# Small VectorE steps of the attention's shifts and output layernorms, queued and issued between row maxima

## The chip, the cores and the metric

The kernel runs on one core of one Trainium2 chip. The metric is the device time of one execution in microseconds. The kernel before took 1540.59 us, the median of three runs (1538.79, 1540.59 and 1546.41).

## What is computed

The reference is a stack of two layers on x with 2 x 1024 tokens of 512 features, all in float32. Each layer has an attention part and a feed-forward part, and each part is put between two layernorms:

```python
x = x + _layernorm(_L0_attn_ref(_layernorm(x), ...))   # per-token attention over feature groups
x = x + _layernorm(_L0_ffn_ref(_layernorm(x), ...))    # weights quantized to -1, 0, 1
x = x + _layernorm(_L1_attn_ref(_layernorm(x), ...))   # causal attention, 16 heads, 4 key/value heads, rope
x = x + _layernorm(_L1_ffn_ref(_layernorm(x), ...))    # gated, 2 of every 4 hidden values kept
```

The change is in the third line. Its core is

```python
logits = jnp.einsum('bhqd,bhkd->bhqk', q, k_ctx) / math.sqrt(dk)     # dk = 32, T = 1024
probs = jax.nn.softmax(logits + mask, axis=-1)
out = jnp.einsum('bhqk,bhkd->bhqd', probs, v_ctx)
return out.transpose(0, 2, 1, 3).reshape(Bx, Tx, D_MODEL) @ c_w.T
```

and then the layernorm of that output is added to x.

## The kernel before, in words

Tokens lie on the 128 partitions, 16 tiles of 128 tokens (8 for each of the two batches), four tiles to a group. The first two parts of the stack run until about 400 us of the profiled execution, the causal attention until about 957 us, and the last feed-forward part from there to the end.

**Tasks and steps of the attention.** A task is one batch b, one group of query tokens Q (0 or 1, 512 tokens each) and one key/value head g (0 to 3, which serves four query heads, REP = 4): 16 tasks. A task passes twice over its scores.

- *Row maxima and sums.* score_step (from L820) takes a tile of 128 queries (ii) and a chunk of up to 512 keys (ch). For each of the four heads TensorE multiplies (L830; the causal mask is added by a small matmul, L836), VectorE takes the negated row maximum from PSUM (L841, tile mxs), and ScalarE computes exponentials with that maximum as bias, keeping only their sum (L845, tile junk).
- *Shifts.* When a task has all its maxima and sums, shifts (from L880) makes of them one number per query and head, the minus logarithm of the denominator. With two key chunks it first combines them (mfin, md, an exponential of md on ScalarE at L890, sfin); minus_log computes a logarithm out of 14 VectorE steps on 128 x 16 values (L860 to L876); in_pieces splits the result into three bf16 pieces (L791 to L794, tile pm). That makes 18 VectorE steps for a task with Q = 0 and 22 for one with Q = 1. maxima_T (pieces_T, L801 and L803) transposes the pieces on TensorE and copies them to mT.
- *Probabilities and values.* prob_step j computes the transposed scores of one tile of 128 keys for the four heads (L906, pst), adds the shift by a short matmul with mT (L913), and ScalarE takes the exponential (L919, pT); GpSimd zeroes what the causal mask forbids (L921). value_step, one step later, multiplies by the values (L935, po) and at the end of a task copies the sum out (L943, oT).

**Output parts.** After the last task of a (b, Q) come output_parts: four products with the output weights (L969, py), for each a copy, bn_stats and bn_aggr on VectorE (L982 to L984), and then add: the inverse root of the variance out of 13 small VectorE steps on 128 x 4 values (inverse_root, L188 to L195), four ln_apply (L199, 128 x 512, tile tmpy) and four additions to x_sb on GpSimd (L962). The last (b, Q) is done tile by tile instead ("alone").

**What sets the order.** The main loop runs over 96 steps, one prob_step each. In a step it issues prob_step, then as many score steps of later tasks as are due (scores_up_to; a value_step goes between the first two heads and the last two), and then what was put on the list due for this step: projections of batch 1's queries, pieces of weights for the next stage, output_parts, maxima_T. Many steps have no score step. The loop stands in a manual schedule for TensorE and GpSimd: their instructions stay in the order of the program. VectorE's and ScalarE's order is chosen by the scheduler of the framework. GpSimd's additions of a layernorm are held back (soon) until the next prob_step has been issued (flush). Scores and transposed scores share a ring of seven PSUM banks, so that a score matmul waits until ScalarE has read the bank that it takes over.

Of the kernel before, what the change touches and what calls it, by code (L numbers as in the profile page):

```python
# [9 lines left out]
F32 = mybir.dt.float32  # L10
# [8 lines left out]
P = 128  # L19
# [5 lines left out]
def two_layer_sandwich(  # L25
# [138 lines left out]
    load_x(2 * GT, NT)  # L164


    def ln_stats(pool, srcs, name, roots=True):

        n = len(srcs)
        st = pool.tile([P, n, 6], F32, tag=f"st{n}", name=f"st_{name}")  # L170
        mv = pool.tile([P, n, 2], F32, tag=f"mv{n}", name=f"mv_{name}", bufs=4)
        rs = pool.tile([P, n], F32, tag=f"rs{n}", name=f"rs_{name}", bufs=4)
        for k, s in enumerate(srcs):
            nc.vector.bn_stats(out=st[:, k, :], in_=s)
            nc.vector.bn_aggr(out=mv[:, k, :], in_=st[:, k, :])
        if roots:
            nc.scalar.activation(rs, mv[:, :, 1], AF.Sqrt, bias=eps_t)
            nc.vector.reciprocal(rs, rs)
            return mv, rs
        return mv, inverse_root(pool, mv, n, name, rs)  # L180

    def inverse_root(pool, mv, n, name, rs=None):

        if rs is None:
            rs = pool.tile([P, n], F32, tag=f"rs{n}", name=f"rs_{name}", bufs=4)
        v = pool.tile([P, 2, n], F32, tag=f"nv{n}", name=f"nv_{name}", bufs=1)
        y = pool.tile([P, n], I32, tag=f"ny{n}", name=f"ny_{name}", bufs=1)
        nc.vector.tensor_scalar(v[:, 0, :], mv[:, :, 1], EPS_LN, None, ALU.add)  # L188
        nc.vector.tensor_scalar(y, v[:, 0, :].bitcast(I32), 1, None, ALU.logical_shift_right)
        nc.vector.tensor_scalar(rs.bitcast(I32), y, -1.0, 1597463007.0, ALU.mult, ALU.add)  # L190
        nc.vector.tensor_scalar(v[:, 0, :], v[:, 0, :], -0.5, None, ALU.mult)
        for _ in range(3):
            nc.vector.tensor_tensor(v[:, 1, :], rs, rs, ALU.mult)
            nc.vector.tensor_tensor(v[:, 1, :], v[:, 1, :], v[:, 0, :], ALU.mult)
            nc.vector.scalar_tensor_tensor(rs, v[:, 1, :], 1.5, rs, ALU.add, ALU.mult)  # L195
        return rs

    def ln_apply(dst, src, mv, rs, k):
        nc.vector.tensor_scalar(  # L199
            dst, src, mv[:, k, 0:1], rs[:, k : k + 1], ALU.subtract, ALU.mult  # L200
        )

    def minus_mean(pool, mv, rs, n):

        nb = pool.tile([P, n], F32, tag=f"nb{n}", name=f"nb{n}", bufs=4)
        nc.vector.scalar_tensor_tensor(nb, mv[:, :, 0], -1.0, rs, ALU.mult, ALU.mult)
        return nb

    def transpose4(src, pt):
# [575 lines left out]
    def in_pieces(m, name):  # L785

        nonlocal n_pm
        pm = pms[n_pm % 2]
        n_pm += 1
        r1 = s1.tile([P, GT, REP], F32, tag="r1", name=f"r1_{name}")  # L790
        nc.vector.tensor_copy(pm[:, :, :, 0], m)  # L791
        nc.vector.tensor_tensor(r1, m, pm[:, :, :, 0], ALU.subtract)
        nc.vector.tensor_copy(pm[:, :, :, 1], r1)
        nc.vector.tensor_tensor(pm[:, :, :, 2], r1, pm[:, :, :, 1], ALU.subtract)  # L794
        return pm

    def pieces_T(pm, name):
# [23 lines left out]
    def score_step(tk, ii, ch, heads):  # L821


        st, g, i = tk.st, tk.g, GT * tk.Q + ii
        k0 = ch * GW
        k1 = min(k0 + GW, (i + 1) * P)
        w = k1 - k0
        for r in heads:
            pa = ring(f"psc_{tk.nm}_{ii}_{ch}_{r}")
            nc.tensor.matmul(  # L830
                pa[:, :w], tk.q.bitcast(F32R)[:, r, ii * P : (ii + 1) * P],
                st.k[ch].bitcast(F32R)[:, g, :w],
                start=True, stop=True,
            )
            if k1 == (i + 1) * P:
                nc.tensor.matmul(  # L836
                    pa[:, w - P : w], identb, cmaskb, start=False, stop=True,
                    skip_group_check=True,
                )
            mx = tk.mx[:, ii, r, ch : ch + 1]  # L840
            nc.vector.tensor_reduce(mx, pa[:, :w], AX.X, ALU.max, negate=True)  # L841
            junk = s1.tile(
                [P, GW], BF16, tag="junk", name=f"junk_{tk.nm}_{ii}_{ch}_{r}", bufs=3
            )
            nc.scalar.activation(  # L845
                junk[:, :w], pa[:, :w], AF.Exp, bias=mx, accum_out=tk.sm[:, ii, r, ch : ch + 1]
            )
# [3 lines left out]
    def minus_log(v, m, name):  # L851


        def tmp(tag, dtype=F32):
            return s1.tile([P, GT, REP], dtype, tag=tag, name=f"{tag}_{name}", bufs=1)

        vi = v.bitcast(I32)
        e, f = tmp("lge", I32), tmp("lgf", I32)
        ef, z, z2, p = tmp("lgw"), tmp("lgz"), tmp("lgy"), tmp("lgp")
        nc.vector.tensor_scalar(e, vi, 23, None, ALU.logical_shift_right)  # L860
        nc.vector.tensor_scalar(
            f, vi, 0x7FFFFF, 0x3F800000, ALU.bitwise_and, ALU.bitwise_or
        )
        fr = f.bitcast(F32)
        nc.vector.tensor_scalar(ef, e, -LN2, 126.5 * LN2, ALU.mult, ALU.add)
        nc.vector.tensor_scalar(z, fr, R2, None, ALU.add)
        nc.vector.reciprocal(z, z)
        nc.vector.scalar_tensor_tensor(z, fr, R2, z, ALU.subtract, ALU.mult)
        nc.vector.tensor_tensor(z2, z, z, ALU.mult)
        nc.vector.tensor_scalar(p, z2, 1.0 / 9.0, 1.0 / 7.0, ALU.mult, ALU.add)  # L870
        nc.vector.tensor_tensor(p, p, z2, ALU.mult)
        nc.vector.scalar_tensor_tensor(p, p, 1.0 / 5.0, z2, ALU.add, ALU.mult)
        nc.vector.scalar_tensor_tensor(p, p, 1.0 / 3.0, z2, ALU.add, ALU.mult)
        nc.vector.scalar_tensor_tensor(p, p, 1.0, z, ALU.add, ALU.mult)
        nc.vector.scalar_tensor_tensor(ef, p, -2.0, ef, ALU.mult, ALU.add)
        nc.vector.tensor_tensor(ef, ef, m, ALU.add)  # L876
        return ef

    def shifts(tk):

        m, sm = tk.mx[:, :, :, 0], tk.sm[:, :, :, 0]
        if tk.Q > 0:
            n = tk.Q + 1
            m = s1.tile([P, GT, REP], F32, tag="mfin", name=f"mfin_{tk.nm}")
            nc.vector.tensor_reduce(m, tk.mx[:, :, :, :n], AX.X, ALU.min)
            d = s1.tile([P, GT, REP, n], F32, tag="md", name=f"md_{tk.nm}")
            nc.vector.tensor_tensor(
                d, m.unsqueeze(3).to_broadcast([P, GT, REP, n]), tk.mx[:, :, :, :n], ALU.subtract
            )
            nc.scalar.activation(d, d, AF.Exp)  # L890
            nc.vector.tensor_tensor(d, d, tk.sm[:, :, :, :n], ALU.mult)
            sm = s1.tile([P, GT, REP], F32, tag="sfin", name=f"sfin_{tk.nm}")
            nc.vector.tensor_reduce(sm, d, AX.X, ALU.add)
        tk.pm = in_pieces(minus_log(sm, m, tk.nm), tk.nm)

    def maxima_T(tk):
        tk.mT = pieces_T(tk.pm, tk.nm)

    def prob_step(tk, j):
# [45 lines left out]
    def output_parts(st, Q):  # L945
# [9 lines left out]
            return s1.tile([P, D], F32, tag=tag, name=f"tmp{nm}_{ii}", bufs=1)  # L955

        def add(tiles, mv, ys):
            rs = inverse_root(s1, mv, n, f"{nm}_{tiles[0]}")
            for k, ii in enumerate(tiles):
                ln_apply(ys[ii], py_of.pop(ii) if alone else ys[ii], mv, rs, k)  # L960
                xt = x_sb[:, st.b * TB + GT * Q + ii, :]
                soon(lambda xt=xt, y=ys[ii]: nc.gpsimd.tensor_tensor(xt, xt, y, ALU.add))  # L962

        py_of, got = {}, []

        def part(ii):
            py = py_of[ii] = ring(f"p{nm}_{ii}")
            for c in range(DC):
                nc.tensor.matmul(  # L969
                    py, st.oT[Q][:, c, ii * P : (ii + 1) * P], wc1[:, c, :],  # L970
                    start=(c == 0), stop=(c == DC - 1),
                )
            ys[ii] = y_of(ii)
            if not got or alone:
                got[:] = [
# [79 lines left out]
    with tc.manual_schedule(engines={mybir.EngineType.PE, mybir.EngineType.Pool}):  # L1055
# [84 lines left out]
        def f1_begin():  # L1140
# [4 lines left out]
            load_unit(1)  # L1145
            f1_first.xT = w1a.tile([P, DC, GW], F32, tag="xT", name="xTg1_0")
            f1_first.xd = w1a.tile([P, 3, 2, HW], F32, tag="xd", name="xdg1_0")
            f1_first.mv, f1_first.rs = ln_stats(s1, [x_sb[:, k, :] for k in range(GT)], "f1_0", roots=False)

        def f1_tile(k):  # L1150
# [24 lines left out]
        for step, (tk, j) in enumerate(t_steps):  # L1175
# [7 lines left out]
            def between():  # L1183
                while waiting:
                    waiting.pop()()

            scores_up_to(wanted(step), step, between)
            between()
            for f in due.pop(step, []):
                f()  # L1190
        values(len(t_steps))
        while due:
            step = min(due)
            flush()
            for f in due.pop(step):
                f()
# [426 lines left out]
```

## Time and profile before

| what | before |
|---|---|
| median of three runs | 1540.59 us |
| the profiled execution, its own time | 1545.5 us |
| its span, first to last instruction | 1543.8 us |
| mean granted TensorE clock | 0.968 |
| 0 to 400 us: TensorE, VectorE, ScalarE, GpSimd busy | 382.3, 234.0, 137.7, 139.5 us |
| 400 to 957 us (attention): the same | 508.2, 373.7, 393.7, 152.2 us |
| 957 us to the end: the same | 575.5, 402.4, 196.9, 28.7 us |
| row maxima (L841) | 384, 551 ns each |
| exponentials of scores (L845) and of pst (L919) | 384 of 630 ns, 384 of 551 ns |
| GpSimd additions of a normed tile (L962) | 16, median 1440 ns |

The table's busy times are sums of the durations of the instructions of an engine in that stretch. A busy TensorE is not TensorE at its full rate, since the clock that is granted to it can be half, and then each matmul takes longer. PE stands for TensorE, PEld for its weight loads, DVE for VectorE, ACT for ScalarE, POOL for GpSimd. A line such as L841 is a line of the kernel before.

### The profile page before, as it was taken

What the parts mean: (1) busy time and instruction counts of PE and PEld (TensorE: products, weight loads), DVE (VectorE), ACT (ScalarE), POOL (GpSimd) and SP (SyncE); (2) the same over time, 40 slices, a digit from 0 to 9 for tenths busy, and PEclk for the clock granted to TensorE, in tenths of its full rate; (3) what the DMA queues carried; (4) which work ended last, traced back from release to release, by engine and by line L of the source; (5) the groups of instructions that cost most, each with busy time, mean ns of one, the idle gap of its engine ahead of it and who ended that gap; (6) DMA issues with size and microseconds to landing.
All of it is one profiled execution on the core that took longest, in us unless ns stands there. A gap on an engine that the chain in (4) does not pass through costs nothing.

```text
span 1543.8 us, 20277 instructions
## 1 busy us (share of the span) xinstructions
PE 1466.0 (95%) x6998; PEld 1051.8 (68%) x6998; DVE 1010.0 (65%) x2303; ACT 728.2 (47%) x1849; POOL 320.4 (21%) x424
## 2 busy tenths in 40 slices
PE   7999999999779999999898999999999999999997
PEld 3558888877545554545444446888888888888886
DVE  5976465652467767657777645786578468846783
ACT  4242343332268757797685983451245034404420
POOL 1104475332303314323432002000100010001001
PEclk9999999999879999998798999999999999999999
DMA  7200211201554343343351002643353345235411
GB/s 293 75 14 28 82 55 42 55 18 52 122 151 101 104 124 89 117 135 74 93 148 57 2 1 88 247 144 143 130 211 117 143 171 191 96 143 205 156 48 75
DMA packets 78870, 167.51 MB, mean 109 GB/s; under 512 B 10224, under 2 KB 35824, under 8 KB 76720
## 3 DMA queue, kind: packets, MB, share of 16 engines
q1 hardware_dynamic: 72928, 148.39, 29.8%
q0 software_dynamic: 4784, 16.52, 2.9%
q10 hardware_dynamic: 1056, 1.31, 0.3%
q8 instruction: 55, 0.90, 0.2%
q14 instruction: 47, 0.39, 0.1%
HBM read 138.94 MB, written 27.26 MB: 108 GB/s over the span
## 4 chain that ended last, share of the span: by engine, by line
PE 76%; DVE 10%; ACT 8%; issue 2%; DMA 2%; POOL 1%; SPq 0%; ACTq 0%; DVEq 0%; POOLq 0%
PE acc L1383 12%; PE ph L371 7%; PE pb_u L1232 7%; PE pb_g L1232 7%; ACT junk L845 5%; PE po L390 4%; PE psc L830 4%; PE pc_g L1232 4%; PE pc_u L1232 4%; PE pst L906 4%; PE py L969 3%; PE pq L248 3%; PE pq L556 3%; PE po L935 3%; DVE mxs L841 3%; ACT pT L919 3%
## 5 line engine op out<-in xcount | busy, mean ns | idle before, releaser
L841 DVE TENSOR_REDUCE mxs<-psc 128x1 f32<-128x512 f32 (+3 forms) x384 | 195.6, 551 | 85.6 <-PE psc L836 43.9
L845 ACT ACTIVATE junk<-psc,mxs 128x512 bf16<-128x512 f32 (+3 forms) x384 | 221.8, 630 | 43.0 <-DVE mxs L841 40.6
L919 ACT ACTIVATE pT<-pst 128x512 f32<-128x512 f32 (+3 forms) x384 | 159.9, 551 | 82.9 <-PE pst L913 82.3
L371 PE MATMUL ph<-xTg,w 128*128 128x512 f32 x704 | 170.2, 395 | 2.1 <-DVE xTg L361 0.9
L830 PE MATMUL psc<-k,q 128*128 128x512 f32 (+3 forms) x384 | 144.8, 452 | 16.5 <-ACT junk L845 6.7
L371 PEld LDWEIGHTS ph<-xTg,w 128*128 128x128 f32 x704 | 132.4, 189 | 30.3 <-DVE xTg L361 1.2
L906 PE MATMUL pst<-q,k 128*128 128x512 f32 (+3 forms) x384 | 126.0, 418 | 19.9 <-ACT junk L845 18.3
L1436 POOL TENSOR_TENSOR x_sb<-x_sb,o 128x512 f32<-128x512 f32 x14 | 19.1, 1363 | 549.2 <-DVE o L199 549.1
L830 PEld LDWEIGHTS psc<-k,q 128*128 128x128 f32 x384 | 77.0, 213 | 79.4 <-ACT pT L919 23.3
L1383 PE MATMUL acc<-wd,h 128*128 128x256 f32 x512 | 121.6, 379 | 0.0
L921 POOL TENSOR_SCALAR_AFFINE_SELECT pT<-pT 128x256 f32<-128x256 f32 x128 | 52.0, 413 | 329.1 <-ACT pT L919 326.9
L906 PEld LDWEIGHTS pst<-q,k 128*128 128x128 f32 x384 | 69.5, 201 | 66.9 <-ACT junk L845 43.6
L1383 PEld LDWEIGHTS acc<-wd,h 128*128 128x128 f32 x512 | 97.0, 190 | 13.1
L845 ACT ACTIVATION_READ_ACCUMULATOR junk<-psc,mxs 128x1 f32 x384 | 97.6, 255 | 0.0
L935 PE MATMUL po<-pT,v 128*32 128x512 f32 (+3 forms) x768 | 92.2, 520 | 1.6 <-POOL pT L921 1.3
L1383 PE MATMUL acc<-wd,hx 128*128 128x256 f32 x384 | 93.3, 379 | 0.0
L380 POOL TENSOR_TENSOR hl<-h,hl 128x512 fp32r<-128x512 f32 x44 | 57.1, 1302 | 156.6 <-ACT hl L379 156.4
L390 PE MATMUL po<-w,hl 128*128 128x512 f32 x352 | 86.7, 390 | 0.6 <-DVE tmp L199 0.6
L377 DVE TENSOR_TENSOR h<-h,ph 128x512 f32<-128x512 f32 x44 | 30.0, 684 | 79.3 <-PE ph L371 69.4
L1383 PEld LDWEIGHTS acc<-wd,hx 128*128 128x128 f32 x384 | 73.0, 190 | 9.9
L1293 DVE TENSOR_TENSOR gate<-gate,ab 128x1024 f32<-128x1024 f32 x32 | 39.2, 1225 | 58.6 <-ACT ab L1290 58.6
L1400 ACT COPY p<-acc 128x512 f32<-128x512 f32 x8 | 4.7, 583 | 152.2 <-PE acc L1383 152.2
(273 smaller groups left out, 2880.5 us busy)
## 6 DMA issues: line engine op xcount, KB each, us to landing
w<-kept SPq DMA_DIRECT2D x64, 512.0 KB, 5.9
q<-dq SPq DMA_DIRECT2D x64, 256.0 KB, 5.0
wd<-keptd SPq DMA_DIRECT2D x16, 1024.0 KB, 8.3
w<-in_f_wg SPq DMA_DIRECT2D x32, 384.0 KB, 3.4
w<-in_f_wu SPq DMA_DIRECT2D x32, 384.0 KB, 5.3
wd<-in_f_wd SPq DMA_DIRECT2D x16, 768.0 KB, 5.9
dq<-hl SPq DMA_DIRECT2D x32, 320.0 KB, 3.3
kept<-wl POOLq DMA_DIRECT2D x16, 512.0 KB, 3.0
```

Of the source, the lines that this page charges most:

```text
L371: nc.tensor.matmul(pa, wt[:, c, cols], xT[:, s, c, :], start=(c == 0 and s == 0), stop=(c == DC - 1 and s == 1),)
L380: nc.gpsimd.tensor_tensor(hl[:, 1, :], h, hl[:, 0, :].bitcast(F32), ALU.subtract)
L390: nc.tensor.matmul(pos0[g][k], hl[:, s, k * P : (k + 1) * P], w3[:, hc, :], start=(hc == 0 and s == 0), stop=(hc == HC - 1 and s == 1),)
L830: nc.tensor.matmul(pa[:, :w], tk.q.bitcast(F32R)[:, r, ii * P : (ii + 1) * P], st.k[ch].bitcast(F32R)[:, g, :w], start=True, stop=True,)
L841: nc.vector.tensor_reduce(mx, pa[:, :w], AX.X, ALU.max, negate=True)
L845: nc.scalar.activation(junk[:, :w], pa[:, :w], AF.Exp, bias=mx, accum_out=tk.sm[:, ii, r, ch : ch + 1])
L906: nc.tensor.matmul(pas[r][:, c0:], st.k[j // GT].bitcast(F32R)[:, g, (j % GT) * P : (j % GT + 1) * P], tk.q.bitcast(F32R)[:, r, c0:], star ...
L919: nc.scalar.activation(p[:, e, c0:], pas[2 * pr + e][:, c0:], AF.Exp)
L921: nc.gpsimd.affine_select(out=p[:, :, c0 : c0 + P], in_=p[:, :, c0 : c0 + P], compare_op=ALU.is_ge, fill=0.0, base=0, pattern=[[0, 2], [1, ...
L935: nc.tensor.matmul(tk.po[DK * r : DK * r + DK, c0:], st.v[j // GT][:, j % GT, g * DK : (g + 1) * DK], tk.pT[j, r // 2][:, r % 2, c0:], sta ...
L1232: nc.tensor.matmul(p, a[:, c, :], b[:, c, :], start=(first and c == 0), stop=(c == 1), skip_group_check=not first,)
L1383: nc.tensor.matmul(acc[m // 2][:, m % 2 * HW : (m % 2 + 1) * HW], a[:, j, k * P : (k + 1) * P], b[:, j, :], start=start, stop=True, skip_g ...
```

## The change

All VectorE steps of a shift go into a queue, shift_drops, in place of being issued at once, with the exponential on ScalarE as an item of it, followed by six empty items. The inverse root and the four applies of an output layernorm (not the "alone" one) go into a second queue, norm_drops. drip(n) takes n items, from shift_drops first and from norm_drops when that is empty. It is called with 2 after every row maximum, and at the end of each step with 2, or with 8 if the step had no scores. Both queues are emptied where somebody needs the result: at the next shifts, at maxima_T, at the next layernorm's first part and its add, and at the end. Each row maximum with its two items, and each drip, stands in a short manual schedule for VectorE, which keeps the order of the steps within it.

```diff
+    class Drops:
+        def __init__(self):
+            self.items = []
+
+        def __getattr__(self, op):
+            return lambda *a, **kw: self.items.append(lambda: getattr(nc.vector, op)(*a, **kw))
+
+        def drain(self, n=None):
+            while self.items and n != 0:
+                f = self.items.pop(0)
+                if f is not None:
+                    f()
+                n = None if n is None else n - 1
+
+    shift_drops, norm_drops = Drops(), Drops()
+
+    def in_order(f):
+        with tc.manual_schedule(engines={mybir.EngineType.DVE}):
+            f()
+
+    def drip(n):
+        for _ in range(n):
+            (shift_drops if shift_drops.items else norm_drops).drain(1)
...
-    def inverse_root(pool, mv, n, name, rs=None):
+    def inverse_root(pool, mv, n, name, rs=None, vec=None):
...
-        nc.vector.tensor_copy(pm[:, :, :, 0], m)
-        nc.vector.tensor_tensor(r1, m, pm[:, :, :, 0], ALU.subtract)
+        shift_drops.tensor_copy(pm[:, :, :, 0], m)
+        shift_drops.tensor_tensor(r1, m, pm[:, :, :, 0], ALU.subtract)
...
             mx = tk.mx[:, ii, r, ch : ch + 1]
-            nc.vector.tensor_reduce(mx, pa[:, :w], AX.X, ALU.max, negate=True)
+            with tc.manual_schedule(engines={mybir.EngineType.DVE}):
+                nc.vector.tensor_reduce(mx, pa[:, :w], AX.X, ALU.max, negate=True)
+                drip(2)
...
     def shifts(tk):
 
+        in_order(shift_drops.drain)
...
-            nc.scalar.activation(d, d, AF.Exp)
-            nc.vector.tensor_tensor(d, d, tk.sm[:, :, :, :n], ALU.mult)
+            shift_drops.items.append(lambda: nc.scalar.activation(d, d, AF.Exp))
+            shift_drops.items += [None] * 6
+            shift_drops.tensor_tensor(d, d, tk.sm[:, :, :, :n], ALU.mult)
...
     def maxima_T(tk):
+        in_order(shift_drops.drain)
         tk.mT = pieces_T(tk.pm, tk.nm)
...
         def add(tiles, mv, ys):
-            rs = inverse_root(s1, mv, n, f"{nm}_{tiles[0]}")
-            for k, ii in enumerate(tiles):
+            in_order(norm_drops.drain)
+            vec = nc.vector if alone else norm_drops
+            rs = inverse_root(s1, mv, n, f"{nm}_{tiles[0]}", vec=vec)
+
+            def apply(k, ii):
                 ln_apply(ys[ii], py_of.pop(ii) if alone else ys[ii], mv, rs, k)
                 xt = x_sb[:, st.b * TB + GT * Q + ii, :]
-                soon(lambda xt=xt, y=ys[ii]: nc.gpsimd.tensor_tensor(xt, xt, y, ALU.add))
+                soon(lambda: nc.gpsimd.tensor_tensor(xt, xt, ys[ii], ALU.add))
+
+            for k, ii in enumerate(tiles):
+                if alone:
+                    apply(k, ii)
+                else:
+                    norm_drops.items.append(lambda k=k, ii=ii: apply(k, ii))
...
+            if ii == 0:
+                in_order(norm_drops.drain)
             ys[ii] = y_of(ii)
...
+            in_order(norm_drops.drain)
             f1_first.mv, f1_first.rs = ln_stats(s1, [x_sb[:, k, :] for k in range(GT)], "f1_0", roots=False)
...
+            before = pos
             scores_up_to(wanted(step), step, between)
             between()
+            n_drops = 2 if pos > before else 8
+            in_order(lambda: drip(n_drops))
             for f in due.pop(step, []):
                 f()
         values(len(t_steps))
+        in_order(shift_drops.drain)
+        in_order(norm_drops.drain)
```

The steps themselves, their tiles and their shapes stay as they were.

## The prediction

> **What bounds the kernel now.** I read the page first, then the granted clock stage by stage, then the waits of the attention stage (about 440 to 940 us), then the timelines of the stretches in which TensorE stood still.
>
> ```profile
> PE 1466.0 (95%) x6998; PEld 1051.8 (68%) x6998; DVE 1010.0 (65%) x2303; ACT 728.2 (47%) x1849; POOL 320.4 (21%) x424
> ```
>
> TensorE is nearly always busy, and the change gives it no matmul less. So the change can win only what TensorE loses to waits and to a lower clock. From 0 to 400 us and from 957 us to the end its busy share is 96% and 98% (382.3 of 400, 575.5 of 587) at a clock of 0.99; from 400 to 957 it is 91% (508.2 of 557) at 0.93. The change works only in this middle part. Two waits carry it:
>
> ```profile
> ACT junk L845 <- DVE mxs L841: 31.4, 27, 5.1
> PE pst L906 <- ACT junk L845: 18.3, 42, 3.9
> ```
>
> Columns: total us, times, longest. ScalarE's exponential of a score row waits for VectorE's row maximum, and TensorE waits for that exponential, because it frees the PSUM bank. The stage by 4 us slices (engine busy, then clock, DMA share, GB/s) shows where the long ones lie:
>
> ```profile
> 752.00:756.00 4.00, 3.33 (x19) 1.69 (x19) 4.00 (x22) 2.99 (x16) 1.49 (x1) 0.85 0.34 89
> 756.00:760.00 4.00, 1.77 (x7) 0.89 (x6) 4.00 (x7) 0.00 (x0) 4.00 (x4) 0.50 0.84 173
> 760.00:764.00 4.00, 2.65 (x9) 1.17 (x9) 2.75 (x5) 3.32 (x9) 3.42 (x6) 0.50 0.00 0
> 764.00:768.00 4.00, 4.00 (x23) 2.48 (x22) 2.31 (x5) 3.45 (x12) 1.50 (x3) 0.50 0.40 136
> ...
> 836.00:840.00 4.00, 1.21 (x10) 0.83 (x8) 3.97 (x7) 0.78 (x2) 2.65 (x3) 1.00 0.00 0
> 840.00:844.00 4.00, 1.58 (x4) 1.15 (x4) 3.90 (x14) 2.80 (x11) 2.91 (x3) 0.52 0.00 0
> 844.00:848.00 4.00, 4.00 (x22) 1.78 (x22) 2.30 (x7) 2.82 (x13) 0.77 (x2) 0.50 0.00 0
> ```
>
> Twice VectorE is full while TensorE (first column) and ScalarE (fourth) stand; afterwards the clock is 0.50, until 772 and about 850. VectorE's timeline says what it did:
>
> ```profile
> 754.89 1.30 DVE L791 CAST pm<-lgw 128x16 bf16<-128x16 f32 x1
> 756.08 0.53 DVE L199 TENSOR_SCALAR tmpy<-tmpy,mv_y,rs_y 128x512 f32<-128x512 f32 x1
> 756.53 1.26 DVE L792 TENSOR_TENSOR r<-lgw,pm 128x16 f32<-128x16 f32 x1
> ...
> 759.31 0.68 DVE L841 TENSOR_REDUCE mxs<-psc 128x1 f32<-128x512 f32 x1
> ...
> 836.76 3.80 DVE L199 TENSOR_SCALAR tmpy<-tmpy,mv_y,rs_y 128x512 f32<-128x512 f32 x4
> ```
>
> Both are output layernorms (b0 Q1, b1 Q0): four applies and, in the first, the last shift steps stand in front of row maxima whose scores are ready. They are slow because GpSimd adds each applied tile to x_sb at the same time (16 adds of 1.44 us median): the cast's median is 0.204 us, here it takes 1.30; four applies take 3.80 where four at the 0.544 median take 2.2.
>
> **The change, part by part.** The matmul order is the same in both built orders. I compare VectorE's order, placing each maximum behind its score matmul.
>
> *Shift chains moved between maxima.* Of 16 chains (18 to 22 VectorE steps), the tails of about five move behind later row maxima, 11 to 20 steps each: some 70 steps, and about 39 small norm steps with them. In the built order they come mostly one by one, not in pairs. Their price is in two places of the trace:
>
> ```profile
> 525.66 0.18 DVE L873 SCALAR_TENSOR_TENSOR lgp<-lgp,lgy 128x16 f32<-128x16 f32 x1
> 525.87 0.17 DVE L874 SCALAR_TENSOR_TENSOR lgp<-lgp,lgz 128x16 f32<-128x16 f32 x1
> ...
> 751.97 0.17 DVE L869 TENSOR_TENSOR lgy<-lgz 128x16 f32<-128x16 f32 x1
> 752.05 0.16 DVE L193 TENSOR_TENSOR nv_y<-rs_y 128x4 f32<-128x4 f32 x1
> ```
>
> In a chain each step starts 0.21 us after the one it needs; put between other work it costs 0.08. So 110 steps cost 110 x 0.08 = 8.8 us of VectorE time instead of 23. But several of these chains ran in steps without scores, where nobody waited (523 to 527 us lies under a query projection of TensorE), and now stand before maxima. VectorE has a third of the stage free (352 of 520 us busy). I put a tenth of the 8.8 on the path: 1 us lost; bounds 0 (all in gaps) and 3.
>
> *b0 Q1's norm.* The new order has no shift cast between the applies, its adds come two mask steps later on GpSimd, and three applies stand in front of the third maximum of a step (3 x 0.54 = 1.6 us, or 2.85 if adds meet them). TensorE is covered there by one value step (1.06) and two scores (0.73) = 1.8. Before: TensorE idle in 752 to 764 is 12 - 3.33 - 1.77 - 2.65 = 4.2 us; at the stage's usual 9% it would be 1.1. Recovered 3.2, left over 0.3 (bounds 0 and 1.1).
>
> *b1 Q0's norm.* Idle in 836 to 844: 8 - 1.21 - 1.58 = 5.2, usual 0.7, so 4.5 to win. In the new order seven chain steps (1.4 us) and four applies (3.80, the adds directly behind) stand between the mT copy and the next maximum. TensorE has four pst (1.45), four short matmuls (0.40) and two scores (0.7) to do first, 2.5, and 1.8 beyond: 5.2 - 4.3 = 0.9 is left (bounds 0 and 2.7).
>
> *b0 Q0's norm.* TensorE's 1.36 us wait at 589 us (for the xT copy, queued between norm steps) goes. But the 3.81 us apply block, which lay ahead of a projection, now stands before a maximum: 0.4 + 3.8 - 4.3 is just covered; I take 0.3, at worst 1.7.
>
> *The clock.* ScalarE did 6.5 us of work in 764 to 772 and 7.3 in the next 8 us at full clock: 0.9 us lost. After the second stall 5.6 against 8.0: 2.4. Together 3.3, if no new stall lowers it (bounds 0 and 5). The Trainium skill, "TensorE: Matmul & The Clock Gate", Part 1, says that the clock halves after an idle window of about 3.4 us and is back after as long a busy one. By that each stall would cost some 1.7 us of work, and leftovers of 0.3 to 0.9 nothing. The trace differs: TensorE worked without a gap from 764 and the clock came back at 772; and it fell to 0.55 in 792 to 796 after waits of only 0.3 to 0.7 us. I take the rows, so leftovers may cost clock too.
>
> *The md exponential* (L890) of four chains goes behind the four pT exponentials of the next step: 4 x 0.55 = 2.2 us that VectorE may stand before L891, with row maxima of no coming step behind, only hl and xT of one projection. I take 0.3 in all; bounds 0 and 4.
>
> *The lock.* "SBUF — State Buffer", Who interferes with whom, says against this change that VectorE and GpSimd hold a port pair for a whole instruction and the second blocks: a small step next to a maximum may then cost 1.1 us more. By the rule alone, at GpSimd's 28% busy, 110 x 0.28 x 0.5 of a GpSimd step of 0.7 would be 11 us (an estimate). The rows say less: L791 to L794 average 311 ns over medians of about 206, 6.7 us over 64 steps, of which 3.8 are those at 755 to 760; nearly 3 us per 60 steps remains. For 110 steps 5 us, a fifth before a waiting maximum: 1.
>
> The layernorm of the next stage is queued later too; its result is first used at 914 us (ptf, L480). DMAs of the stage's pieces keep their order but for one weight load; I put 0.
>
> Sum: 3.2 + 4.5 + 1.4 + 3.3 = 12.4 to win; less 0.3 + 0.9 + 0.3 left over, 1 + 0.3 + 1 of cost: 8.6. The profiled execution took 1545.5 us (span 1543.8) and would take 1537; it lies 4.9 above the median of 1540.6, so 1532 on that scale.
>
> **The rivals.** *Half given back* (0.25): ScalarE is nearly full where TensorE is not held (4.00 of 4 in 852 to 860), so a recovered stall only brings the next exponential wait forward, and the clock dips elsewhere, as at 702 to 712 without any block. Half of 8 us: 1537. For it: 18.3 us of waits lie in 42 pieces; against: the two blocks are the only long ones. *The spread isn't done* also ends here: the built order leaves chains of b1's first long task at 783 to 789 as one block.
>
> *A new block in front of maxima* (0.22), slower than before: the applies stay together. Behind mT in b0 Q0 and b1 Q0 they cost their upper bounds, 1.7 + 2.7, each lowers the clock as at 840 (2.4 each), and lock and md reach 5 + 4, interleaving 3: 21 lost against the 12.4 won: 9 slower, 1549. It decides once what is lost exceeds 12.4. Against it: a 3.81 us block at 591 us cost TensorE no wait at all.
>
> **How the numbers follow.** My forecast, 1525 to 1536, has 0.53; half given back 0.25; the block 0.22. The range 1524 to 1547 leaves two in ten out. About 0.5% (7.7 us) can be told from no change: below 1532.9 lies some 0.46, above 1548.3 0.18, the rest 0.36.
>
> **What would show it.** Right: no slice after 750 in which VectorE is full and ScalarE empty, L791 below 250 ns on average, the clock of 400 to 957 us at 0.95 or more, "ACT junk waits for DVE mxs" below 22 us. Wrong: the same wait at 30 or more, with the applies (L199 tmpy) in front of a maximum and a clock of 0.5 behind them, or new waits of TensorE for pm or mT.

## The result and the profile after

The kernel after takes 1537.59 us (median of 20 runs, 1534.35 to 1540.95); the kernel before, run beside it, 1543.06 (20 runs, 1536.67 to 1546.41). The ratio is 0.9968, 95% interval 0.9958 to 0.9977: 5 us faster. I had forecast 8.6 us less than the earlier median of 1540.6, so 1532. The direction is right. The size is not: 1537.6 lies above the 1525 to 1536 of my own forecast, beside the 1537 of the rival "half given back", and inside only the outer range of 1524 to 1547.

The page of the kernel after, busy time of each engine:

```profile
PE 1458.7 (95%) x6998; PEld 1049.4 (68%) x6998; DVE 1007.8 (66%) x2303; ACT 729.4 (48%) x1849; POOL 319.7 (21%) x424
```

TensorE does the same work and is 7.3 us less "busy", partly since fewer of its matmuls run at half clock. The waits of its attention stage, 440 to 940 us (total us, times, longest), first three of before that the prediction does not show, then those of after:

```profile
DVE md L891 <- ACT md L890: 7.7, 8, 1.5
...
PE pmt L801 <- DVE pm L794: 1.9, 1, 1.9
...
PE pst L913 <- DVE mT L803: 0.4, 2, 0.2
```

```profile
PE pst L940 <- ACT junk L876: 14.8, 36, 2.3
...
DVE md L174 <- ACT md L922: 12.8, 7, 3.5
ACT junk L876 <- DVE mxs L871: 11.4, 19, 2.3
...
PE pmt L830 <- DVE pm L174: 4.1, 3, 2.0
...
PE pst L947 <- DVE mT L832: 1.9, 2, 1.4
```

ScalarE's wait for row maxima fell from 31.4 to 11.4 us, as wished; but VectorE's wait for the md exponential rose from 7.7 to 12.8, TensorE's for pm from 1.9 to 4.1 and for mT from 0.4 to 1.9. The spread steps are all recorded under L174, the line of the queue's lambda.

The profiled execution of after (1534.4 us, span 1532.7) is 11.1 us below that of before, twice what the medians say. To see where, I take from both traces the 16 copies of a task's finished po into oT (the COPY oT<-po rows of VectorE's timeline) as marks; a stretch named 0_1_2 (batch, Q, head group) runs from the copy before it to its own. After is 5.3 us ahead already at the first mT copy, where hardly a moved step has run: that is between two executions, not of the change (in the twelve kernels below this copy comes at 448.1 to 454.4 us; before has it at 454.6, after at 449.3). From the first oT copy to the last it is 5.7 us shorter, near what the medians say, and for the other kernels below the sums of these stretches follow the medians within 3.5 us. The last two columns are the time in the stretch in which TensorE is idle, and the time in which its granted clock is 0.50, before and after. In us:

| stretch | before | after | difference | forecast | TensorE idle | at half clock |
|---|---|---|---|---|---|---|
| 0_0_1 to 0_0_3 | 71.5 | 73.1 | +1.6 | 1 + 1 for interleaving and lock, all stretches | 4.3, 4.8 | 3.4, 6.8 |
| 0_1_0 and 0_1_1 (b0 Q0's norm) | 103.1 | 107.3 | **+4.2** | -1.4 + 0.3 | 6.2, 6.5 | 0, 13.7 |
| 0_1_2 (a chain with md) | 27.3 | 30.3 | **+2.9** | +0.3 for all md | 1.2, 2.9 | 0, 3.0 |
| 0_1_3 | 35.2 | 31.3 | **-3.9** | nothing | 0.8, 0.5 | 10.2, 0.4 |
| 1_0_0 to 1_0_3 (b0 Q1's norm) | 88.5 | 80.1 | -8.4 | -3.2 + 0.3 - 0.9 | 8.5, 5.3 | 23.9, 6.8 |
| 1_1_0 and 1_1_1 (b1 Q0's norm) | 85.3 | 83.0 | -2.3 | -4.5 + 0.9 - 2.4 | 7.7, 5.8 | 13.7, 13.7 |
| 1_1_2 and 1_1_3 | 46.9 | 47.1 | +0.1 | | 1.3, 1.5 | 0, 0 |

So 14.6 us were won and 8.8 lost again. At b0 Q0 TensorE's idle time hardly grew: its same 498 matmuls take 3.8 us longer, and its clock is at half for 13.7 us, in before never. The two rows of this stretch (length, then each engine's busy time and its instructions, then the clock), before and after:

```profile
546.90:650.00 103.10, 96.92 (x498) 50.07 (x498) 74.14 (x196) 69.77 (x207) 34.79 (x52) 1.00 0.35 96
```

```profile
543.10:650.40 107.30, 100.76 (x498) 52.69 (x498) 75.99 (x196) 70.74 (x207) 35.44 (x53) 0.94 0.34 94
```

The losses in detail. Slices of 4 us of after (columns as in the prediction):

```profile
600.00:604.00 4.00, 2.79 (x10) 1.76 (x8) 4.00 (x9) 2.28 (x8) 4.00 (x4) 0.50 0.00 0
604.00:608.00 4.00, 3.85 (x16) 1.10 (x15) 3.06 (x5) 2.97 (x9) 3.60 (x6) 0.50 0.77 230
...
836.00:840.00 4.00, 1.98 (x15) 0.97 (x7) 4.00 (x6) 1.74 (x4) 3.96 (x3) 1.00 0.01 2
840.00:844.00 4.00, 2.95 (x15) 0.96 (x15) 3.31 (x10) 3.49 (x12) 1.61 (x2) 0.69 0.00 0
```

The rows at 600 are new; those at 836 are b1 Q0's old stall, smaller. The stall at 752 to 764 is gone. After's timeline at b0 Q0:

```profile
594.67 0.40 PE L830 MATMUL pmt<-identb,pm 128*128 128x128 bf16 x4
594.75 1.28 POOL L617 TENSOR_TENSOR ra<-ra,rbq 128x512 f32<-128x512 f32 x1
...
594.90 1.15 DVE L174 TENSOR_TENSOR nv_y<-nv_y 128x4 f32<-128x4 f32 x1
...
597.31 0.41 DVE L832 COPY mT<-pmt 128x512 bf16<-128x512 bf16 x1
...
597.77 0.40 PE L947 MATMUL pst<-mT,onesb 32*128 32x512 bf16 x4 [1.37 <-DVE mT L832]
...
598.02 3.84 DVE L228 TENSOR_SCALAR tmpy<-tmpy,mv_y,rs_y 128x512 f32<-128x512 f32 x4
...
602.29 0.47 ACT L876 ACTIVATE junk<-psc,mxs 128x256 bf16<-128x256 f32 x1 [1.57 <-DVE mxs L871]
...
602.90 2.19 PE L940 MATMUL pst<-q,k 128*128 128x512 f32 x3 [1.21 <-ACT junk L876]
```

Here mT comes late (1.37). It is ready to be copied at 595.1, but a norm step of 128 x 4 values ahead of it, one of those that the queue put there, takes 1.15 us beside a GpSimd addition, and two maxima follow. Then the applies, which stand behind this copy, hold the next maxima (1.57 for ScalarE, 1.21 for TensorE). TensorE's clock is at half from 599.2 for 10.2 us, and for 3.4 us more from 643.6. At 0_1_2:

```profile
670.22 0.48 ACT L922 ACTIVATE md<-md 128x32 f32<-128x32 f32 x1
...
670.73 0.37 DVE L174 TENSOR_TENSOR md<-md,sms 128x32 f32<-128x32 f32 x1 [3.50 <-ACT md L922]
...
677.32 0.40 PE L830 MATMUL pmt<-identb,pm 128*128 128x128 bf16 x4 [1.80 <-DVE pm L174]
...
680.05 2.06 ACT L953 ACTIVATE pT<-pst 128x512 f32<-128x512 f32 x4 [4.58 <-PE pst L947]
```

md's input is written at 667.2, but ScalarE reaches the exponential at 670.2, behind four pT. The chain's other 20 steps stand behind it, so TensorE waits 1.80 us for pm and ScalarE 4.58 for TensorE.

### The profile page after: what moved, and what is told of

It is laid out like the page before. It is cut to its first block, busy times and chain, and to the rows that moved or that the text cites. A ratio compares the mean times of both kernels' runs of the same rounds, so it can differ in the third digit from the quotient of the medians.

```text
span 1532.7 us, 20280 instructions
## 1 busy us (share of the span) xinstructions
PE 1458.7 (95%) x6998; PEld 1049.4 (68%) x6998; DVE 1007.8 (66%) x2303; ACT 729.4 (48%) x1849; POOL 319.7 (21%) x424
## 4 chain that ended last, share of the span: by engine, by line
PE 78%; DVE 10%; ACT 6%; issue 2%; DMA 2%; POOL 2%; SPq 0%; DVEq 0%; ACTq 0%; POOLq 0%
PE acc L1434 13%; PE pb_g L1283 7%; PE pb_u L1283 7%; PE ph L400 7%; PE psc L859 4%; PE po L419 4%; ACT junk L876 4%; PE pst L940 4%; PE py L1012 4%; PE pc_g L1283 4%; PE pc_u L1283 4%; PE pq L585 3%; PE pq L277 3%; PE po L969 3%; DVE mxs L871 3%
## 5 line engine op out<-in xcount | busy, mean ns | idle before, releaser
L871 DVE TENSOR_REDUCE mxs<-psc 128x1 f32<-128x512 f32 (+3 forms) x384 | 199.1, 551 | 72.7 <-PE psc L865 38.8
```

## The experiments

The theories as they stood: A, the applies still stand as blocks in front of maxima, stretched by the additions; B, the md exponential is late; C, ScalarE hands back what is won. The stretches of the table are those of the table above, in us.

| kernel | ratio to before, 95% interval | 0_1_0+1 | 0_1_2 | 0_1_3 | 1_0_x | 1_1_0+1 |
|---|---|---|---|---|---|---|
| before | 1 | 103.1 | 27.3 | 35.2 | 88.5 | 85.3 |
| after | 0.9968 (0.9958 to 0.9977) | 107.3 | 30.3 | 31.3 | 80.1 | 83.0 |
| e1 additions late | 0.9958 (0.9944 to 0.9973) | 106.3 | 30.3 | 31.6 | 80.9 | 81.7 |
| e2 before, additions late | 1.0009 (0.9994 to 1.0024) | 106.5 | 27.4 | 31.8 | 87.7 | 84.4 |
| e3 md at once | 0.9938 (0.9922 to 0.9954) | 103.0 | 27.4 | 31.2 | 84.0 | 82.2 |
| e4 shifts only | 1.0024 (1.0012 to 1.0036) | 106.8 | 30.3 | 31.6 | 86.5 | 86.5 |
| e5 md at once, late chains | 0.9946 (0.9930 to 0.9963) | 106.7 | 27.3 | 31.2 | 80.2 | 82.3 |
| e6 md at once, early chains | 0.9950 (0.9930 to 0.9970) | 103.4 | 30.3 | 31.5 | 80.9 | 82.5 |
| e7 norms only | 1.0001 (0.9988 to 1.0013) | 105.0 | 27.3 | 35.3 | 86.5 | 82.1 |
| e8 md at once, additions late | 0.9919 (0.9903 to 0.9935) | 103.0 | 28.1 | 31.2 | 82.9 | 81.9 |
| e9 md at once, empty items kept | 0.9981 (0.9967 to 0.9995) | 109.8 | 27.3 | 31.1 | 80.9 | 82.6 |
| e10 md queued, no empty items | 0.9967 (0.9955 to 0.9979) | 106.8 | 30.5 | 31.3 | 80.1 | 81.7 |
| e11 free order | 0.9984 (0.9971 to 0.9996) | 106.3 | 30.2 | 32.5 | 80.6 | 83.8 |
| e12 e8 with parted applies | 0.9911 (0.9898 to 0.9924) | 103.9 | 27.4 | 31.2 | 80.1 | 80.9 |

**e1 and e2: the additions.** The same edit on after (shown, without the part that issues what is left at the end) and on before:

```diff
-    def flush():
+    late = []
+
+    def flush(tick=0):
+        for e in late:
+            e[0] -= tick
+        while late and late[0][0] <= 0:
+            late.pop(0)[1]()
         while waiting_adds:
...
-                soon(lambda: nc.gpsimd.tensor_tensor(xt, xt, ys[ii], ALU.add))
+                add_x = lambda: nc.gpsimd.tensor_tensor(xt, xt, ys[ii], ALU.add)
+                late.append([8, add_x]) if not alone else soon(add_x)
...
             prob_step(tk, j)
-            flush()
+            flush(1)
```

> The kernel after, with GpSimd's additions of the normed tiles put eight steps later in its queue; VectorE's order stays. Theory A (the gain is lost where the four applies stand as one block before row maxima, stretched by the additions beside them, and where the clock is halved behind them): the blocks at 598 and 835 us shrink from 3.84 and 3.83 us to about 2.2, TensorE's waits for the exponentials there (1.2, and 2.3 + 0.8) fall by about 1.6 each, part of the half clock at 600 to 608 and 840 to 848 goes: 3 to 6 us less than after (1537.6), ratio to before about 0.994. Theory B (the gain is lost in the delayed exponential of the maxima's differences and so in the wait of TensorE for pm): no change, ratio 0.997. Theory C (ScalarE fills what is won and hands it back elsewhere): at most 1 us less, ratio 0.996 to 0.997.

> The kernel before, with only GpSimd's additions put eight steps later; nothing is queued or spread. Theory A: the casts at 755 us fall from 1.3 to 0.2 us and the applies at 837 from 3.8 to 2.2; some 3 us of b0 Q1's stall and 1.6 of b1 Q0's go, with part of the half clock behind them: 4 to 7 us less, ratio 0.9955 to 0.9975, as much as the whole change gave. Theory B: the change's gain came from moving steps, the additions are no matter: ratio 0.999 to 1. Theory C: recovered stalls are handed back: ratio 0.998 to 1.

e1 gave 1535.85 us, 1.7 less than after's median with overlapping intervals: less than A's 3 to 6, though the blocks of four applies at b0 Q0 and b1 Q0 take 1.91 us each, TensorE's wait at b1 Q0 is 0.91 in place of 2.31, and 0_1_0+1 and 1_1_0+1 became 1.0 and 1.35 us shorter. In e2 the additions leave b0 Q1's block (its two pm casts take 0.45 and 0.73 in place of 1.30 and 1.26) and 1_0_1 falls from 21.9 to 18.8 us, but the time stays. Its timeline shows where the additions went:

```profile
632.01 4.95 POOL L968 TENSOR_TENSOR x_sb<-x_sb,tmpy 128x512 f32<-128x512 f32 x4
632.11 1.22 DVE L799 CAST pm<-r 128x16 bf16<-128x16 f32 x1
...
639.15 0.47 PE L836 MATMUL psc<-k,q 128*128 128x512 f32 x1 [1.78 <-DVE rbq L590]
...
782.95 4.95 POOL L968 TENSOR_TENSOR x_sb<-x_sb,tmpy 128x512 f32<-128x512 f32 x4
783.04 1.22 DVE L880 SCALAR_TENSOR_TENSOR lgp<-lgp,lgz 128x16 f32<-128x16 f32 x1
...
785.53 1.19 DVE L882 TENSOR_TENSOR lgw<-lgw,mfin 128x16 f32<-128x16 f32 x1
...
789.59 0.69 ACT L851 ACTIVATE junk<-psc,mxs 128x512 bf16<-128x512 f32 x1 [4.89 <-DVE mxs L847]
```

They now run beside a shift chain whose steps wait on each other, and each such step takes as long as an addition, 1.2 in place of 0.2 us; ScalarE waits 4.89. At 632 us the statistics of the added tiles (st_f) come late with them, in front of the rope steps of a projection (rbq); TensorE waits 1.78, then runs at half clock for 10.2 us, and 0_1_1 takes 50.0 in place of 45.0. The cost was moved from one block to another: the additions are cheap only where no small VectorE steps stand in front of work that TensorE waits for. A's claim that the lock relief alone equals the change falls.

**e3, e5, e6: the exponential at once.** e3 issues the first two steps of the chain and the exponential directly; e5 does so for tasks from 0_1_2 on (tk.n >= 6), e6 for those before.

```diff
-            shift_drops.tensor_reduce(m, tk.mx[:, :, :, :n], AX.X, ALU.min)
+            nc.vector.tensor_reduce(m, tk.mx[:, :, :, :n], AX.X, ALU.min)
...
-            shift_drops.tensor_tensor(
+            nc.vector.tensor_tensor(
...
-            shift_drops.items.append(lambda: nc.scalar.activation(d, d, AF.Exp))
-            shift_drops.items += [None] * 6
+            nc.scalar.activation(d, d, AF.Exp)
```

> The kernel after, with the chain's first two steps and the exponential of the maxima's differences issued at once as before; the rest is still queued. Theory B: VectorE's wait for that exponential falls from 12.8 us to about 7.7, TensorE's wait for pm at 677 us (1.8) and the gap at 676 to 680 go: 2 to 4 us less, ratio about 0.995. Theory A: the built order also moves three of b0 Q0's applies ahead of a projection, so the stall and half clock at 600 to 608 go (1.2 + about 2 us): 3 less, but the slices around 677 give under 1. The time alone does not tell them apart, the slices do. Theory C: within 1 us of after.

> The kernel after, with the exponential of the maxima's differences (and the two steps before it) issued at once only for the tasks from 0_1_2 on, so that the earlier chains, and b0 Q0's applies behind mT, stay as after. Theory B (that exponential, waiting behind four pT, makes pm late): the 2.9 us that the stretch from 0_1_1's to 0_1_2's output copy became longer (27.3 to 30.3) go, so 3 us less than after, ratio about 0.995. Theory A (b0 Q0's block at 598 us): as after, 0.9968, within 1 us; the stretches of 0_1_0 and 0_1_1 stay at 59.3 and 48.0 us.

> The kernel after, with the same exponential issued at once only for the tasks before 0_1_2; in the built order this brings b0 Q0's first three applies ahead of a projection, as in the kernel with all of them at once, and leaves the rest as after. Theory A: the stretches of 0_1_0 and 0_1_1 fall from 59.3 and 48.0 to about 56.9 and 46.1: 4.3 us less than after, ratio about 0.994. Theory B: the stretch of 0_1_2 stays at 30.3 and the time as after, 0.9968, within 1 us.

1532.77, 1532.44 and 1533.58 us. The intervals of e5 and e6 overlap that of after, so the stretches decide. Each half gave what its theory said, in its own stretch and not in the other's: e5 brings 0_1_2 back to 27.3 and leaves 106.7; e6 brings 0_1_0+1 to 103.4 and leaves 30.3. e5's timeline at the place shown above:

```profile
669.41 0.45 ACT L924 ACTIVATE md<-md 128x32 f32<-128x32 f32 x1
...
669.89 0.19 DVE L174 TENSOR_TENSOR md<-md,sms 128x32 f32<-128x32 f32 x1 [1.55 <-ACT md L924]
...
676.66 0.40 PE L830 MATMUL pmt<-identb,pm 128*128 128x128 bf16 x4
```

The exponential starts 1.25 us after the start of the step before it (in after 3.17), and TensorE no longer waits for pm there. e6's timeline at b0 Q0's norm:

```profile
592.26 1.46 DVE L228 TENSOR_SCALAR tmpy<-tmpy,mv_y,rs_y 128x512 f32<-128x512 f32 x3
592.56 1.89 PE L590 MATMUL pkv<-wkv,xT 128*128 128x256 f32 x8
```

Three applies now run under a key and value projection of TensorE. In e6 TensorE is at half clock for 3.4 us in 0_1_0+1, in after for 13.7. Both losses of the change thus hang on one edit, the exponential as an item of the queue with six empty ones behind it: it delays its own chain, and, since norm_drops waits until shift_drops is empty, the longer queue also pushes b0 Q0's applies a step on, into the step where mT is due. e3 does not reach the sum of the two (0.9928), but its interval holds it; its stretch 1_0_2 took 18.4 us where e5, with the same VectorE order from there on, took 15.7: the clock was 0.72 in place of 1.00.

**e9 and e10: exponential or empty items.** e9 is e3 with the six empty items, e10 is after without them.

```diff
 e9
             nc.scalar.activation(d, d, AF.Exp)
+            shift_drops.items += [None] * 6
 e10
             shift_drops.items.append(lambda: nc.scalar.activation(d, d, AF.Exp))
-            shift_drops.items += [None] * 6
```

> The kernel after, with the exponential of the differences and the two steps before it at once, but the six empty items kept in the queue. In the built order b0 Q0's four applies then stand behind four maxima and in front of the mT copy. If the exponential's place behind four pT is what made 0_1_2's stretch longer (27.3 to 30.3 us), it is 27.3 here; if the empty items did it, 30.3. The applies of 3.8 us in front of mT: TensorE waits there, so 0_1_0 and 0_1_1 together stay near after's 107.3 (103 without a loss). Time by that 3 us less than after, ratio about 0.995.

> The kernel after without the six empty items; the exponential is still queued. In the built order b0 Q0's applies stand two by two between the four maxima of a step. If the exponential's place made 0_1_2 longer, it stays at about 30.3 us; if the empty items did, it falls to 27.3. Theory A: with the block parted, 0_1_0 and 0_1_1 together fall from 107.3 to about 103: 3 to 4 us less than after, ratio 0.9945; if only the total of VectorE's work in that stretch counts, no change there, 0.9968.

1538.51 and 1537.98 us. 0_1_2 is 27.3 with the exponential at once, and 30.5 with it queued, whatever the empty items: in all 14 kernels, it is at most 28.1 in the one case and at least 30.2 in the other. At b0 Q0 I was wrong twice: e9 lost more than expected (109.8), and parting the applies two by two (e10) did not help (106.8). The empty items alone, or the queued exponential alone, are enough for that loss. The waits of e9, then of e10, tell why:

```profile
PE pst L947 <- DVE mT L832: 5.4, 2, 5.0
```

```profile
PE pst L946 <- DVE mT L832: 3.0, 3, 2.4
```

What ends last in e9 and e10 is not the next maximum but the mT copy, which stands behind all four applies however they are parted (in after the applies stand behind it). Theory A is refined: it is not the block's shape, but whether it lies ahead of a deadline (mT, or a maximum with scores ready) or under a projection.

**e4 and e7: half the change.** e4 sets `vec = nc.vector` and calls `apply(k, ii)` at once for all norms; e7 replaces shift_drops by an object that passes each step to nc.vector at once, and issues the exponential at once too (that line is not shown).

```diff
 e4
-            vec = nc.vector if alone else norm_drops
+            vec = nc.vector
...
-                if alone:
-                    apply(k, ii)
-                else:
-                    norm_drops.items.append(lambda k=k, ii=ii: apply(k, ii))
+                apply(k, ii)
 e7
+    class Now:
+        items = []
+
+        def __getattr__(self, op):
+            return getattr(nc.vector, op)
+
+        def drain(self, n=None):
+            return None
+
+    shift_drops = Now()
```

> The kernel after, with the layernorms' inverse root and applies issued at once as before, only the shift steps queued. Theory A: b0 Q0's block stands two maxima earlier as before and cost no wait there (3 us less than after), b0 Q1's four applies stand together before a step's first maximum with the additions beside them (3 to 4 more), b1 Q0's behind the first maximum as before (1 to 2 more): 1 to 3 us slower than after, ratio 0.998 to 0.999. Theory B: as after, 0.997. If the spread of the shift steps were worth nothing, 1.0.

> The kernel after, with the shift steps issued at once as before and only the inverse root and applies queued. Theory A: b0 Q0's applies stand ahead of a projection (no loss there), the exponential of the differences is in time, but b0 Q1's block with the shift casts between its applies is back behind a first maximum: 4 us slower than the kernel with that exponential at once (1532.8), ratio 0.996 to 0.998. If spreading the shift steps was worth nothing: ratio 0.994. If it was worth the whole gain: 1.0.

1545.62 and 1542.18 us: e4 is slower than before, which no theory had expected, e7 as before. Alone neither frees b0 Q1: 1_0_x stays at 86.5 in both, and is 80 to 81 where both are queued (84.0 and 82.9 in e3 and e8); TensorE is idle there for 8.1 and 10.5 us in e4 and e7, for 4.4 to 5.9 in the others that have both queues. In e4 b1 Q0's stretch is the longest of all (86.5), and b0 Q0's stays at 106.8, where I had expected no wait. At both places a queued shift step now stands between the applies and the maxima and meets an addition:

```profile
596.21 1.23 DVE L174 TENSOR_TENSOR lgp<-lgp,lgy 128x16 f32<-128x16 f32 x1
...
598.90 1.99 PE L590 MATMUL pkv<-wkv,xT 128*128 128x256 f32 x8 [1.78 <-ACT junk L876]
```

In before the wait there is shorter:

```profile
596.32 1.99 PE L561 MATMUL pkv<-wkv,xT 128*128 128x256 f32 x8 [0.62 <-ACT junk L845]
```

At 842.85 another such step takes 1.23, and TensorE waits 5.06 (before 3.92).

**e11: without the fixed order.** The two manual schedules for VectorE (around a maximum with its two items, and in in_order) are taken away.

```diff
-            with tc.manual_schedule(engines={mybir.EngineType.DVE}):
-                nc.vector.tensor_reduce(mx, pa[:, :w], AX.X, ALU.max, negate=True)
-                drip(2)
+            nc.vector.tensor_reduce(mx, pa[:, :w], AX.X, ALU.max, negate=True)
+            drip(2)
...
-        with tc.manual_schedule(engines={mybir.EngineType.DVE}):
-            f()
+        f()
```

> The kernel after with its two queues and their places, but without the manual schedules for VectorE: the scheduler may move the steps again. In the built order the shift steps go back in front of maxima in long runs, the applies of b0 Q1 stay two by two. If the fixed order is what keeps the shift steps apart and the shift steps matter (as with the norm alone, 1.000): ratio 0.999 to 1.0. If the applies' parting is enough: 0.996 to 0.997.

1539.74 us, between the two expectations; its interval overlaps after's. The places in the queue alone bring 1_0_x to 80.6; the medians of e11 and after differ by 2 us, and these runs do not settle whether the fixed order adds anything.

**e8 and e12: a faster kernel.** e8 is e3 with the edit of e1. e12 adds three empty items behind each apply:

```diff
-                    norm_drops.items.append(lambda k=k, ii=ii: apply(k, ii))
+                    norm_drops.items += [lambda k=k, ii=ii: apply(k, ii), None, None, None]
```

> The kernel after, with the exponential of the differences at once and GpSimd's additions eight steps later. Theory A: the applies' blocks take 2.2 in place of 3.8 us; b1 Q0's stretch (1_1_0) falls from 48.3 to about 46.5, b0 Q0's by under 1: 1.5 to 2.5 us less than with the exponential alone (1532.8), ratio about 0.9925. If the additions beside the applies cost nothing: 0.9938, as there. If the moved additions stand in front of selects that TensorE waits for: slower than that.

> The kernel with the exponential at once and the additions late (ratio 0.9919), and three empty items behind each apply: in the built order the applies of b0 Q1 and b1 Q0 stand one by one behind maxima. Theory A: what is left of b1 Q0's block (1_1_0 at 45.6 us, a half clock behind it) goes, and some at b0 Q1: 1 to 2 us less, ratio 0.991. Theory C (ScalarE fills what is won): 0.992, as there.

1529.21 and 1529.28 us: both beat before by 13 us and after by 8. e8's applies at b1 Q0, without additions beside them:

```profile
828.66 1.90 DVE L228 TENSOR_SCALAR tmpy<-tmpy,mv_y,rs_y 128x512 f32<-128x512 f32 x4
...
831.26 0.69 ACT L882 ACTIVATE junk<-psc,mxs 128x512 bf16<-128x512 f32 x1 [1.65 <-DVE mxs L877]
```

Four applies take 1.90 us, not 3.83. Parting them further (e12) changed nothing that can be told.

## Why the prediction was partly wrong, step by step

- **b0 Q1's norm: right, and too small.** The stall at 752 to 764 is gone. TensorE's idle time fell by 3.2 us, where I had 2.9. With the clock behind it I had 3.8 us to win; 1_0_0 to 1_0_3 became 8.4 us shorter, 3.8 in 1_0_1 itself and 3.9 in the two after it, where the clock is 1.00 and 0.90 in place of 0.82 and 0.80. It needs both queues (e4, e7). I had taken the half clock for the stall's: it starts at 754.8, and TensorE's long wait at 757.8. In after it starts too (752.8), behind waits of 0.27 to 0.34 us, but lasts 3.4 us in place of 17.1.
- **b0 Q0's norm: the step that failed.** "0.4 + 3.8 - 4.3 is just covered; I take 0.3, at worst 1.7". It lost 4.2 (e6 wins 3.9 of it back), where I had 1.1 to win. The wait for xT is gone. In its place TensorE waits 1.21 for the exponential behind the applies, where I took 0.3, and 1.37 for mT: I had summed TensorE's cover for the maximum and not asked for mT, nor for a norm step beside an addition ahead of its copy. Together its idle time grew by 0.4 us. The rest is the term that I put at nothing: "if no new stall lowers it" was said of the clock, and 13.7 us at half clock came, worth at most 6.8 us of TensorE's work (an estimate: half of it). That the new waits set it off is argued from the times; what is shown is that in e3, e6 and e8, where three of the four applies lie under the projection, it is 3.4 us. "A 3.81 us block at 591 us cost TensorE no wait at all" was also misread: behind it TensorE waits 0.62 us at 595.7, for an exponential that the block held up.
- **The md exponential: mis-sized, 2.9 where I took 0.3** (bounds 0 and 4). "With row maxima of no coming step behind" was true; what stands behind is the rest of the chain, and TensorE for pm (1.80 us), with 3.4 us at half clock behind it. e5 shows it.
- **b1 Q0's norm: right in kind, too large.** 6.0 forecast, 2.3 measured: TensorE's wait of 2.31 us for the exponential at 840 is left where I had 0.9, and the clock falls again behind it (0.69, then 0.50 until 848):

```profile
840.29 0.50 PE L940 MATMUL pst<-q,k 128*128 128x512 f32 x1 [2.31 <-ACT junk L876]
```

  I had let all the lost clock come back while a wait was left over; the stretch has 13.7 us at half clock before and after. (The two clock terms are 0.8 and 2.4, so 3.2: 6.5 and 7.3 differ by 0.8, not 0.9.)
- **A gain I had not seen: 0_1_3, 3.9 us.** I took the dip at 702 to 712 for one "without any block" and used it for a rival. Slices of half a microsecond of before:

```profile
698.00:698.50 0.50, 0.19 (x2) 0.00 (x0) 0.50 (x4) 0.08 (x1) 0.00 (x0) 1.00 0.00 0
698.50:699.00 0.50, 0.07 (x1) 0.07 (x1) 0.50 (x3) 0.50 (x3) 0.00 (x0) 1.00 0.00 0
...
700.50:701.00 0.50, 0.50 (x3) 0.30 (x3) 0.00 (x0) 0.50 (x5) 0.00 (x0) 0.50 0.00 0
...
710.50:711.00 0.50, 0.50 (x4) 0.30 (x2) 0.19 (x1) 0.50 (x2) 0.00 (x0) 1.00 1.10 201
```

  One wait of 0.74 us (TensorE, behind shift steps in front of maxima, VectorE full) is followed by 10 us at half clock. e7, with that chain in place, has it too (35.3); e2, with as much idle TensorE time in that stretch (0.83 us, before 0.82), does not (31.8, clock 1.00). The eleven kernels that queue the shift steps are all at 31.1 to 32.5, with at most 1.2 us at half clock there; of the three that do not queue them, before and e7 are at 35.2 and 35.3, e2 at 31.8. So most of this gain may be a matter of when the wait falls, and it is not shown that the change removes it for good.
- **Interleaving and the lock: small in sum, as forecast, but not at each place.** 0_0_1 to 0_0_3 became 1.6 us longer, but 0.9 and 1.2 of it are in e7 and e2 too, which move no shift step. The pm casts from lgw average 246 ns, from 318. Where one small step beside an addition stands ahead of a deadline it costs a microsecond, as at 594.9 us in after and at 596.2 and 842.9 in e4.
- **The sum.** Between the first and the last mark TensorE's idle time fell by 2.6 us; the terms that I had for waits and costs come to 5.3; these 2.7 us are most of what the forecast is too large by. The time at half clock fell by 6.8 us, worth at most 3.4, and I had 3.3. That this agrees is luck: it fell in 1_0_0 to 1_0_3 and in 0_1_3 by 27 us, worth at most 13, where I had 0.9 and nothing; it came anew at b0 Q0 (13.7 us), where I had nothing; and it stayed at b1 Q0, where I had 2.4 to win.
- **The tests.** Right: the wait of junk for mxs (11.4, below 22), the casts below 250 ns, no slice with VectorE full and ScalarE empty. Wrong: the clock of 400 to 957 us is 0.93, not 0.95; and two of the signs that I had named for the wrong case are there, the waits for pm and mT, and applies before a maximum with a clock of 0.50 behind.
- **The rivals.** The size is that of "half given back". Its clock did dip elsewhere, at b0 Q0; but that ScalarE being full hands a recovered stall back is not what held the time up, since e3, which moves one exponential, and e8, which moves the additions too, win on. It was the third rival's mechanism at one place, with the md term beside it, short of the 12.4 at which it would have decided.

## What to carry to other kernels

When small steps are queued to be issued later, leave out of the queue the item that another engine must do: behind that engine's next four long operations it makes the whole chain late. Place a block of VectorE work by what is due behind it on its queue, here the mT copy as well as the maxima, and put it under matmuls that need nothing from it; parting it does not help if the deadline stands behind all its parts. An operation that is moved off one chain's side (the additions) must be followed to the chain that it now lies beside. And when a new wait of TensorE is weighed, the half clock that may follow belongs to its price.

## What the runs showed of the hardware

- Half clock comes in lots of 3.4 us. In all 14 kernels every stretch at half clock that starts between 450 and 940 us is 3.4, 6.8, 10.2 or 17.1 us long. That is the window of the Trainium skill, "TensorE: Matmul & The Clock Gate", Part 1, which says that it runs free; in the prediction I had seen only that the page's rule did not fit. What differs is what sets it off: not a whole idle window; idle times of as little as 0.4 us (e8, at 708) to 2 us in all stand in the 4.5 us ahead of most. What makes it one lot or three stays open.
- From 440 to 940 us before is at half clock for 66 us, after for 53, e8 for 43 (the sum of 1 - clock over these slices, doubled). Before's 66 us are worth at most 33 us of TensorE's work (an estimate: half of them); TensorE is idle for 35 us in that time. The clock can cost about as much as the waits, and its price depends on when they fall.
- A VectorE step of 0.2 us that needs the one before it takes 1.2 us beside a GpSimd addition of 1.24 (e2, 783 to 787 us); in after one of 128 x 4 values takes 1.15 beside an addition of 1.28 (594.9 us). Four applies of 128 x 512 take 3.83 beside additions, 1.90 without (after, e8).
